# Layer 3's row maximum fused with its masked product, int8 masks from ScalarE, and layer 2's source scores spread through HBM

## The chip, the cores and the metric

The kernel runs on one core of one Trainium2 chip. The metric is the device time of one execution in microseconds (us). All sizes are fixed: a batch of 16 graphs with 1024 nodes each and 128 features a node, in float32.

The names of the engines are those of the profile: PE is TensorE's matrix multiply, PEld its weight load, DVE is VectorE, ACT is ScalarE, POOL is GpSimd, and SP is SyncE, which here issues most of the DMAs. A line number such as L1189 is a line of the kernel before.

## The reference, cut to what matters

Four graph layers in a row, each with a layer norm and a relu ahead of it and a residual sum behind it. `adj` is symmetric in its pattern but not in its values; all its entries are zero or between 0.05 and 1.

```python
# layer 2 (attention by source and destination scores)
h = einsum('bnf,fo->bno', hn, W)
s1 = h @ a[:f]
s2 = h @ a[f:]
alpha = tanh(s1[:, :, None] + s2[:, None, :])
attn = softmax(where(adj > 0, alpha, NEG_INF), axis=-1)
last_h = einsum('bij,bjf->bif', attn, h)

# layer 3 (gated attention)
h = einsum('bnf,of->bno', hn, W_w) + W_b
e = einsum('bil,bkl->bik', h @ A, h)
e = e + swapaxes(e, 1, 2)
att = where(adj > 0, e, 0)
att = softmax(att, axis=1) * adj
h_prime = relu(einsum('bij,bjk->bik', att, h))
...
return o_c * tanh(sigmoid(i_c * h_prime + f_c * hn))
```

Layer 0 is three graph convolutions with cosine weights, and layer 1 a neighbour sum with a two-layer perceptron. They aren't touched by the change.

## The kernel before

**Tiling.** One graph is worked on as 8 blocks of 128 nodes. An adjacency matrix is held as 8 tiles `adjT` of 128 x 1024, transposed while it is loaded (a strided DMA, then a DVE transpose, then an ACT copy that also sums the row). A matrix of 1024 x 1024 scores is made a row of blocks at a time: for block row `j`, `Square.row` computes the upper triangle with matmuls (`sq`, L760) and fills the lower one with TensorE transposes of what ACT copied out before (`above`, L792 and L770), or, for most batches, from a round trip through HBM (`by_hbm` and `got`). Every product is two halves of 512 columns (`HALVES`).

**Layer 3, per row block** (`layer3`, L1136, the loop at L1169). DVE multiplies each half of the scores in PSUM by `adjT > 0` (L1177, `scalar_tensor_tensor` with `is_gt` and `mult`) into a chunk `e`. DVE takes the maximum of the whole row with the sign turned (L1189, `top`). ACT computes exp with that bias and the row's sum (L1193). DVE multiplies by `adjT` (L1202; POOL does it for a few rows of the second last batch, L1198), DVE inverts the sum (L1207), ACT scales the block of features (`hs`, L1211), and TensorE accumulates (L822).

**Layer 2's source scores** (`layer2`, L1028). The projection `h` has 130 columns: 128 features, `s1` and `s2`. ACT's tanh needs `s1` of all nodes along the free dimension, the same on each partition. So TensorE transposes, for each of the 8 blocks, the one column of `s1` broadcast to 128 columns (`along`, L1087 to L1092), and ACT evicts the two halves into `s1` (L1093, through the helper at L622). A branch under a flag "S" that sends the scores through HBM is in the code and not switched on.

**What sets the order.** Nothing is issued as it is written. Each piece of work is recorded as an `Op` with an engine, a price in us, and what it reads and writes. `Plan.order` (L137) then goes through time as a list scheduler would: of the ops that are ready on the engine that can start first, it takes the one with the smallest rank, and it gives buffers their slots. The rank is

```python
lead = self.leads.get(o.key + o.edge, self.leads.get(o.key, 0.0))
o.rank = (self.deadline(o.batch) - o.tail - lead, o.seq)
```

where `tail` is the priced work behind the op and `LEADS` is a table of numbers (L347 to L467) by layer, engine and tile, with extra entries for the first two and the last two batches (`<0`, `<1`, `>1`, `>0`). Ops of a batch may start while an earlier batch is unfinished, up to `AHEAD` = 2 batches. The emitted program is then fixed: each engine runs its own list in order, SP's DMAs among them, and waits on semaphores. `POOLS` and `KINDS` say how many slots each kind of buffer has and how many of them later batches may hold.

`FLAGS` (L264) switches variants; `far` (L523) says for which batches the mirrored half goes through HBM (batches 1 to 13).

Of the kernel before, what the change touches and what calls it, by code (L numbers as in the profile page):

```python
# [9 lines left out]
U8 = mybir.dt.uint8  # L10
AF = mybir.ActivationFunctionType
# [12 lines left out]
FLOOR = 1e-30  # L24

# [197 lines left out]
def tile_adj_preln(  # L223
# [40 lines left out]
    FLAGS = set("CabcdkxhyzTG")  # L264
# [61 lines left out]
    for load_it in first:  # L326
# [11 lines left out]
    POOLS = {"adjT": 16, "adjL": 5, "x": 3, "big": 13, "above": 2, "got": 1, "bank": 8, "small": 29, "row": 6, "hbm": 3, "hrow": 2}  # L338
# [4 lines left out]
        "hrow": ("hrow", 2, 1),  # L343
    }
    PERIOD, LAST, AHEAD, WINDOW = 60.0, 52.0, 2, 0.05

    LEADS = {  # L347
        "0 ACT hT": -1, "0 DVE hn": -8, "0 DVE mv": 42.5, "0 DVE nb": -20, "0 DVE st": -77.5, "0 PE ps": -72.5,
        "0 POOL rstd": -1, "00 ACT above": -10.5, "00 ACT hT": 95, "00 ACT hTn": -20.5, "00 ACT sq": -31,
        "00 DMA by": -13.5, "00 DMA got": 15.5, "00 DVE above": -135, "00 DVE ew": 79.5, "00 DVE h": -95.5,  # L350
        "00 DVE ss": -131.5, "00 PE acc0": -252.5, "00 PE ps": -142, "00 PE psP": -0.5, "00 PE sq": -18.5,
        "00 POOL rn": -129.5, "01 ACT above": 56, "01 ACT hT": 11.5, "01 ACT hTn": 15, "01 ACT sq": 15.5,
        "01 DMA by": 4.5, "01 DMA got": 18.5, "01 DVE above": 4.5, "01 DVE ew": 51.5, "01 DVE h": -2.5,
        "01 DVE ss": 16, "01 PE acc0": -164.5, "01 PE ps": 42, "01 PE psP": -5.5, "01 PE sq": -11,
        "02 ACT above": -2, "02 ACT hTn": -615, "02 ACT sq": -25.5, "02 DMA by": 63.5, "02 DMA got": 0.5,
        "02 DVE above": 43.5, "02 DVE ew": -232.5, "02 DVE ss": 79.5, "02 DVE x": -55.5, "02 PE acc0": -28.5,
        "02 PE ps": 12.5, "02 PE sq": 222, "02 POOL rn": -103, "1 ACT g": -33, "1 ACT hn": 66, "1 ACT y1": -7.5,
        "1 DMA adjL": -113, "1 DVE adjL": -21, "1 DVE hn": 1.5, "1 DVE mv": 237.5, "1 DVE nb": 46,
        "1 DVE st": -625.5, "1 DVE x": -0.5, "1 PE acc1": 4, "1 PE py": -167.5, "1 PE py2": 67,
        "1 POOL rstd": -43, "2 ACT e2": -24, "2 ACT h": 287.5, "2 ACT hfl": 53, "2 ACT hn": -13.5,  # L360
        "2 ACT hnT": 18, "2 ACT s1": -14, "2 DVE alone": -51.5, "2 DVE e2": 48.5, "2 DVE h": 20,
        "2 DVE hn": 48.5, "2 DVE hrow": -43.5, "2 DVE mv": -2.5, "2 DVE nb": 78, "2 DVE rden": 9.5,
        "2 DVE x": 10, "2 PE acc2": 108.5, "2 PE p1": -90, "2 PE pf": -26.5, "2 PE ps": 117.5, "2 PE psP": -315,
        "2 POOL rstd": 4.5, "3 ACT above": -19.5, "3 ACT e3": 96.5, "3 ACT gate": -185.5, "3 ACT h3T": 19.5,
        "3 ACT hn": -84.5, "3 ACT hnT": -9.5, "3 ACT hp": -5, "3 ACT hpT": 41, "3 ACT hs": 46.5, "3 ACT z": 25,
        "3 DMA by": -13.5, "3 DMA got": 0.5, "3 DMA z": -130.5, "3 DVE e3": -363.5, "3 DVE gate": 83,
        "3 DVE h": -111.5, "3 DVE hn": 69, "3 DVE mv": -2, "3 DVE nb": 147, "3 DVE st": -192, "3 DVE sum": 53.5,
        "3 DVE top": -84, "3 DVE z": -925, "3 PE acc3": -130.5, "3 PE pg": -18.5, "3 PE ps": 19,
        "3 PE psN": 114, "3 PE psP": 95, "3 PE sq": -0.5, "3 POOL rstd": -59, "3 POOL z": 0.5,
        "T ACT adjT": 1.5, "T DMA adjT": -140.5, "T DVE adjT": -391, "x DMA x": 54.5, "0 ACT hT <0": -2,  # L370
        "0 ACT hT >1": -4.5, "0 ACT hn <1": -4.5, "0 DVE hn <0": 8.5, "0 DVE hn <1": 8.5, "0 DVE hn >0": 15.5,
        "0 DVE hn >1": 1, "0 DVE mv <0": -4.5, "0 DVE mv <1": 113, "0 DVE mv >0": 47.5, "0 DVE mv >1": -25.5,
        "0 DVE nb <0": 101.5, "0 DVE nb <1": -62.5, "0 DVE nb >0": -49, "0 DVE nb >1": -18.5,
        "0 DVE st <0": -85, "0 DVE st <1": -73.5, "0 DVE st >0": -122.5, "0 DVE st >1": -32, "0 PE ps <0": 85.5,
        "0 PE ps <1": 36, "0 PE ps >0": -31, "0 PE ps >1": 40, "0 POOL rstd <0": -6.5, "0 POOL rstd <1": -26,
        "0 POOL rstd >0": -7, "0 POOL rstd >1": 15.5, "00 ACT above <0": -32, "00 ACT above <1": -88,
        "00 ACT above >0": -294, "00 ACT above >1": -3, "00 ACT hT <0": 147.5, "00 ACT hT <1": -7,
        "00 ACT hT >0": 21, "00 ACT hT >1": 161.5, "00 ACT hTn <0": -70.5, "00 ACT hTn <1": 119.5,
        "00 ACT hTn >0": -22, "00 ACT hTn >1": -11, "00 ACT sq <0": -34, "00 ACT sq <1": 134.5,
        "00 ACT sq >0": -119, "00 ACT sq >1": -25.5, "00 DMA by <1": 0, "00 DMA got <1": 1,  # L380
        "00 DVE above <1": -197, "00 DVE ew <0": 180, "00 DVE ew <1": 13, "00 DVE ew >0": -125,
        "00 DVE ew >1": -147.5, "00 DVE h <0": -25.5, "00 DVE h <1": -4.5, "00 DVE h >0": 12,
        "00 DVE h >1": -50.5, "00 DVE params <0": 171, "00 DVE ss <0": 0, "00 DVE ss <1": -73.5,
        "00 DVE ss >0": -46.5, "00 DVE ss >1": -4, "00 PE acc0 <0": -39.5, "00 PE acc0 <1": -212,
        "00 PE acc0 >0": -327.5, "00 PE acc0 >1": -253.5, "00 PE params <0": 56.5, "00 PE ps <0": -18.5,
        "00 PE ps <1": -16, "00 PE ps >0": -32, "00 PE ps >1": -130.5, "00 PE psP <0": -2.5, "00 PE psP <1": 32,
        "00 PE psP >0": -22.5, "00 PE psP >1": -43, "00 PE sq <0": 28.5, "00 PE sq <1": 10, "00 PE sq >0": 3.5,
        "00 PE sq >1": 10, "00 POOL rn <0": -11, "00 POOL rn <1": -164.5, "00 POOL rn >0": -96.5,
        "00 POOL rn >1": -144, "01 ACT above <0": 113, "01 ACT above <1": -11, "01 ACT above >0": 65.5,
        "01 ACT above >1": 24, "01 ACT hT <0": -15, "01 ACT hT <1": -17.5, "01 ACT hT >0": 3.5,  # L390
        "01 ACT hT >1": -39, "01 ACT hTn <0": 16.5, "01 ACT hTn <1": -22, "01 ACT hTn >0": 68,
        "01 ACT hTn >1": 8, "01 ACT sq <0": 174, "01 ACT sq <1": -3.5, "01 ACT sq >0": -69, "01 ACT sq >1": 107,
        "01 DMA by <1": -9, "01 DMA got <1": 25, "01 DVE above <1": -5, "01 DVE ew <0": 140,
        "01 DVE ew <1": -13.5, "01 DVE ew >0": -9.5, "01 DVE ew >1": -34, "01 DVE h <0": -6, "01 DVE h <1": -6,
        "01 DVE h >0": -4.5, "01 DVE h >1": 43.5, "01 DVE ss <0": -13.5, "01 DVE ss <1": 1,
        "01 DVE ss >0": 17.5, "01 DVE ss >1": 106, "01 PE acc0 <0": -17, "01 PE acc0 <1": -31,
        "01 PE acc0 >0": 10.5, "01 PE acc0 >1": 25.5, "01 PE ps <0": 46, "01 PE ps <1": 51, "01 PE ps >0": -56,
        "01 PE ps >1": 82, "01 PE psP >1": 6, "01 PE sq <0": 0, "01 PE sq <1": -6, "01 PE sq >0": 23.5,
        "01 PE sq >1": -25, "02 ACT above >0": -3.5, "02 ACT hTn <0": -145.5, "02 ACT hTn <1": -452.5,
        "02 ACT hTn >0": -65.5, "02 ACT hTn >1": -373.5, "02 ACT sq <0": -8.5, "02 ACT sq <1": -43,  # L400
        "02 ACT sq >0": -58, "02 ACT sq >1": -22.5, "02 DMA by <1": 47.5, "02 DMA got <1": 4,
        "02 DVE above <1": 36.5, "02 DVE ew <0": -5, "02 DVE ew <1": -72, "02 DVE ew >0": -202.5,
        "02 DVE ew >1": -44, "02 DVE ss <0": 70, "02 DVE ss <1": 60.5, "02 DVE ss >0": 39, "02 DVE ss >1": 58,
        "02 DVE x <0": -115, "02 DVE x <1": -125.5, "02 DVE x >0": 0, "02 DVE x >1": -173.5,
        "02 PE acc0 <0": -46.5, "02 PE acc0 <1": -209, "02 PE acc0 >0": 0, "02 PE acc0 >1": -96.5,
        "02 PE ps <0": -241.5, "02 PE ps <1": -295.5, "02 PE ps >0": -48, "02 PE ps >1": -28,
        "02 PE sq <0": -33.5, "02 PE sq <1": -145, "02 PE sq >0": 89, "02 PE sq >1": 0.5, "02 POOL rn <0": 47.5,
        "02 POOL rn <1": -39, "02 POOL rn >0": -118.5, "02 POOL rn >1": -53, "1 ACT g <0": 23, "1 ACT g <1": 48,
        "1 ACT g >0": 25.5, "1 ACT g >1": -35, "1 ACT hn <0": 57.5, "1 ACT hn <1": 189, "1 ACT hn >0": -5.5,
        "1 ACT hn >1": -4.5, "1 ACT y1 <0": 10.5, "1 ACT y1 <1": 13.5, "1 ACT y1 >0": -26.5,  # L410
        "1 ACT y1 >1": 10.5, "1 DMA adjL <0": -772.5, "1 DMA adjL <1": 0, "1 DMA adjL >0": 39,
        "1 DMA adjL >1": -7.5, "1 DVE adjL <0": 42.5, "1 DVE adjL <1": 201.5, "1 DVE adjL >0": -10.5,
# [1022 lines left out]
```

## Time and profile before

| what | value |
|---|---|
| median of three runs | 2436.25 us (2435.44 to 2436.89) |
| profiled execution, first to last instruction | 2432.9 us |
| mean granted TensorE clock | 0.996 of full speed |
| PE matmuls | 11946 |
| DVE busy, ACT busy, POOL busy | 2107.7, 1288.8, 245.1 us |
| moved by DMA | 263.35 MB, mean 108 GB/s |

How to read it: busy time is the time in which an engine had at least one instruction at work, over the whole span. The matmuls of a trace overlap, and their ends are modelled, so what one costs is read from the distance of two starts. The profile's waits name the instruction that came last before an engine went on; an engine that isn't the bottleneck may wait at no cost. All three runs are within 1.5 us.

### The profile page before, as it was taken

To read this page: it belongs to the slowest core of one execution; us is meant where nothing else is said; L and a number is where in the kernel's file an instruction comes from. 1 tells how busy PE (TensorE), PEld (TensorE's weight loads), DVE (VectorE), ACT (ScalarE), POOL (GpSimd) and SP (SyncE) were. 2 spreads that over 40 slices of the span, in tenths; PEclk is the share of its full clock that TensorE was granted. 3 is DMA by queue.
4 is the path that set the end of the run, shared out by engine and by line. 5 is a ranking of instruction groups with operands and counts; after the bars stand their busy time and mean duration, and the time that the engine had idled before them with its cause. 6 is when DMAs were issued, how large, how long until landed. Compare 5 with 4: busy or idle time off the path is not lost. (4 is left out here: it accounts for less than half of the span.)

```text
span 2432.9 us, 34859 instructions
## 1 busy us (share of the span) xinstructions
PE 2387.8 (98%) x11946; PEld 1589.5 (65%) x11946; DVE 2107.7 (87%) x5264; ACT 1288.8 (53%) x2404; POOL 245.1 (10%) x166
## 2 busy tenths in 40 slices
PE   6999999999999999999999999999999999999996
PEld 3568576675767657676675767757576675765763
DVE  6758989889998988999888998998999888897676
ACT  5316564645646465554744646455454644656275
POOL 3001010100101101010010101001011010100011
PEclk9999999999999999999999999999999999999998
DMA  9531927549295573936639285473936738063000
GB/s 149 111 104 36 173 53 148 130 88 171 62 165 121 103 155 81 166 86 136 142 80 180 53 164 130 92 151 80 165 103 122 155 75 151 18 94 89 27 1 18
DMA packets 1126321, 263.35 MB, mean 108 GB/s; under 512 B 970016, under 2 KB 1109552, under 8 KB 1126144
## 3 DMA queue, kind: packets, MB, share of 16 engines
q1 hardware_dynamic: 1108368, 251.73, 52.9%
q10 hardware_dynamic: 16944, 8.52, 1.2%
q8 instruction: 94, 1.54, 0.3%
q0 software_dynamic: 832, 0.88, 0.3%
q14 instruction: 83, 0.68, 0.1%
HBM read 198.14 MB, written 62.91 MB: 107 GB/s over the span
## 5 line engine op out<-in xcount | busy, mean ns | idle before, releaser
L959 DVE SCALAR_TENSOR_TENSOR ew<-sq,rn,adjT 128x512 f32<-128x512 f32 x612 | 432.3, 739 | 83.3 <-ACT above L792 45.6
L822 PE MATMUL acc<-ew,h 128*128 128x512 f32 x1024 | 477.9, 593 | 2.1 <-DVE ew L959 2.1
L760 PE MATMUL sq<-hTn 128*128 128x512 f32 (+3 forms) x1152 | 432.8, 488 | 0.7 <-DVE above L782 0.4
L792 ACT COPY above<-sq 128x256 f32<-128x256 f32 (+3 forms) x432 | 168.2, 394 | 448.5 <-PE sq L760 248.7
L760 PEld LDWEIGHTS sq<-hTn 128*128 128x128 f32 x1152 | 201.4, 192 | 155.2 <-issue 103.9
L822 PEld LDWEIGHTS acc<-ew,h 128*128 128x128 f32 x1024 | 178.9, 190 | 161.8 <-issue 124.0
L833 PEld LDWEIGHTS acc<-h,ew 128*128 128x128 f32 x2048 | 240.8, 192 | 22.6 <-issue 18.8
L833 PE MATMUL acc<-h,ew 128*128 128x128 f32 x2048 | 250.3, 276 | 0.0
L822 PE MATMUL acc<-e,hs 128*128 128x512 f32 x512 | 242.1, 597 | 5.3 <-DVE e L1202 4.1
L833 PEld LDWEIGHTS acc<-h,e 128*128 128x128 f32 x2048 | 232.9, 192 | 11.9 <-issue 6.5
L833 PE MATMUL acc<-h,e 128*128 128x129 f32 x2048 | 233.8, 275 | 1.2 <-DVE e L1109 1.2
L822 PE MATMUL acc<-adjL,hn 128*128 128x512 f32 x512 | 233.5, 593 | 0.3 <-ACT hn L726 0.3
L562 POOL TENSOR_TENSOR rstd<-ve,mhalf 128x8 f32<-128x8 f32 x64 | 105.2, 1643 | 1237.1 <-DVE ve L681 1237.1
L1193 ACT ACTIVATE e<-e,top 128x1024 f32<-128x1024 f32 x128 | 147.0, 1149 | 133.8 <-DVE top L1189 131.8
L770 PEld LDWEIGHTS sq<-ident,above 128*128 128x128 f32 x960 | 125.7, 141 | 125.6 <-issue 89.0
L890 ACT ACTIVATE adjT<-adjT 128x1024 f32<-128x1024 f32 x128 | 135.0, 1055 | 137.2 <-DVE adjT L887 94.5
L770 PE MATMUL sq<-ident,above 128*128 128x128 f32 x960 | 175.1, 273 | 2.0 <-ACT above L792 2.0
L705 ACT ACTIVATE hn<-x,nb,rstd 128x128 f32<-128x128 f32 x256 | 105.3, 482 | 122.8 <-DVE nb L689 115.2
L1109 DVE SCALAR_TENSOR_TENSOR e<-adjT,e 128x512 f32<-128x512 f32 x256 | 158.8, 681 | 9.3 <-ACT e L1105 8.7
L887 DVE STREAM_TRANSPOSE adjT<-adjT 128x1024 f32<-128x1024 f32 x128 | 154.7, 1224 | 11.7 <-DMA adjT<-in_adj_dram 11.0
L782 DVE STREAM_TRANSPOSE above<-sq 128x512 f32<-128x512 f32 x208 | 146.5, 707 | 17.2 <-PE sq L760 17.1
L1202 DVE TENSOR_TENSOR e<-e,adjT 128x512 f32<-128x512 f32 x248 | 161.2, 681 | 0.0
(149 smaller groups left out, 3512.0 us busy)
## 6 DMA issues: line engine op xcount, KB each, us to landing
adjT<-in_adj_dram SPq DMA_DIRECT2D x512, 128.0 KB, 4.0
adjL<-in_adj_dram SPq DMA_DIRECT2D x128, 512.0 KB, 5.0
by_hbm<-above SPq DMA_DIRECT2D x104, 512.0 KB, 3.7
got<-by_hbm SPq DMA_DIRECT2D x416, 128.0 KB, 3.0
x<-in_x_dram SPq DMA_DIRECT2D x15, 512.0 KB, 4.6
out_dram<-z ACTq DMA_DIRECT2D x15, 512.0 KB, 5.6
x<-in_x_dram SPq DMA_DIRECT2D x2, 256.0 KB, 4.9
out_dram<-z ACTq DMA_DIRECT2D x2, 256.0 KB, 2.2
```

The source lines that it names most:

```text
L760: lambda: nc.tensor.matmul(dst.t[:, (first - lo) * P :], cols(leftT.t, j), span(rightT.t, first, hi), start=True, stop=True),
L770: nc.tensor.transpose(cols(dst.t, r), cols(above.t, p), ident)
L782: lambda: nc.vector.transpose(span(above.t, p, p + 4), read.t),
L792: lambda: nc.scalar.copy(span(above.t, p, p + hi - first), read.t[:, (first - lo) * P :]),
L822: lambda s=s, lo=lo, hi=hi: nc.tensor.matmul(acc[s].t, cols(h.t, at, w), span(ew.t, lo, hi), start=(j == 0), stop=(j == NB - 1)),
L833: nc.tensor.matmul(a.t[:, (c - lo) * n : (c - lo + 1) * n], cols(ew.t, c), h.t[:, at * w : at * w + n], start=(j == 0 and c == lo), stop=( ...
L887: dve(V(N), [t], [t], lambda t=t: nc.vector.transpose(t.t, t.t), True)
L890: lambda t=t, c=c: nc.scalar.activation(t.t, t.t, AF.Copy, accum_out=su.t[:, c : c + 1]),
L959: lambda view=view, ew=ew, rn=rn, j=j, lo=lo, hi=hi: nc.vector.scalar_tensor_tensor(by_block(span(ew.t, lo, hi), D, 4), view(), rn.t[:, j ...
L1109: lambda e=e, j=j, lo=lo, hi=hi: nc.vector.scalar_tensor_tensor(span(e.t, lo, hi), span(aT[j].t, lo, hi), 0.0, span(e.t, lo, hi), op0=ALU. ...
L1193: lambda e=e, top=top, tot=tot: nc.scalar.activation(e.t[:, 0:N], e.t[:, 0:N], AF.Exp, bias=top.t, accum_out=tot.t),
L1202: lambda e=e, j=j, lo=lo, hi=hi: nc.vector.tensor_mul(span(e.t, lo, hi), span(e.t, lo, hi), span(aT[j].t, lo, hi)),
```

## The change

The variants "m" and "r" are switched on, two kinds of buffer are added, and the table of leads is a new one.

```diff
-    FLAGS = set("CabcdkxhyzTG")
+    FLAGS = set("CabcdkxhyzTGmr")
...
-    POOLS = {"adjT": 16, "adjL": 5, "x": 3, "big": 13, "above": 2, "got": 1, "bank": 8, "small": 29, "row": 6, "hbm": 3, "hrow": 2}
+    POOLS = {"adjT": 16, "adjL": 5, "x": 3, "big": 13, "above": 2, "got": 1, "bank": 8, "small": 29, "row": 6, "hbm": 3, "hrow": 2, "mask": 5, "dot": 12}
...
-        "hrow": ("hrow", 2, 1),
+        "hrow": ("hrow", 2, 1), "mask": ("mask", 5, 5), "dot": ("dot", 12, 9),
     }
-    PERIOD, LAST, AHEAD, WINDOW = 60.0, 52.0, 2, 0.05
+    PERIOD, LAST, AHEAD, WINDOW = 60, 52, 2, 0.05
```

*Leads.* Every entry of `LEADS` is replaced. `T`, `x`, `0` to `3` and `00` to `02` stand for the loads and layers; a few entries of each:

```diff
-        "0 ACT hT": -1, "0 DVE hn": -8, "0 DVE mv": 42.5, "0 DVE nb": -20, "0 DVE st": -77.5, "0 PE ps": -72.5,
+        "T DMA adjT": 112, "T DVE adjT": -341, "T ACT adjT": -97, "x DMA x": 338, "0 DVE st": -634.5,
+        "0 DVE mv": 268, "0 POOL rstd": 48, "0 DVE nb": -455, "0 DVE hn": -381.5, "0 ACT hn": -11,
...
```

*Layer 3, for all batches.* ACT turns each row of `adjT` into a mask of 0 and 1 in int8 with two instructions, Sign and then Relu. DVE's masked product becomes one `tensor_tensor_reduce` a half, which multiplies mask and scores, writes `e`, and gives the half's maximum (`peak`). The maximum over 1024 elements becomes one over the two halves' values. `top`, `peak` and `sum` move from the kind `small` to the new kind `dot`.

```diff
+            top = dot(f"top_{b}_{j}", 1)
+            if "m" in FLAGS:
+                mask = Buf("mask", [P, N], f"mask_{b}_{j}")
+                act(
+                    S(N), [aT[j]], [mask],
+                    lambda mask=mask, j=j: nc.scalar.activation(mask.t, aT[j].t, AF.Sign),
+                )
+                act(S(N), [mask], [mask], lambda mask=mask: nc.scalar.activation(mask.t, mask.t, AF.Relu))
+                peak = dot(f"peak_{b}_{j}", 2)
...
+                    dve(
+                        V(HALF) + 0.06, [blk(mask, lo, hi), p], [blk(e, lo, hi), blk(peak, s, s + 1, 1)],
+                        lambda e=e, view=view, mask=mask, peak=peak, s=s, lo=lo, hi=hi: nc.vector.tensor_tensor_reduce(
+                            by_block(span(e.t, lo, hi), D, 4), by_block(span(mask.t, lo, hi), D, 4), view(), 1.0, LOWEST,
+                            op0=ALU.mult, op1=ALU.max, accum_out=peak.t[:, s : s + 1],
+                        ),
+                        p is square.got,
+                    )
...
+                dve(
+                    TINY, [peak], [top],
+                    lambda peak=peak, top=top: nc.vector.tensor_reduce(
+                        top.t, peak.t, axis=AX.X, op=ALU.max, negate=True
+                    ),
+                )
```

*Layer 2, for all batches but the last.* One transpose turns the eight columns of `s1` into 8 rows of 128, ACT copies them to SBUF, SP stores them to HBM (4 KB) and loads them back as one row for all 128 partitions (512 KB written). The loop with the eight transposes and two evictions is then left by a `break`; batch 15 still runs it.

```diff
+        if "r" in FLAGS and b < B - 1:
+            pt, sr = ps(f"pt_{b}"), rowbuf(f"sr_{b}")
+            pe(
+                TR, [h], [pt],
+                lambda: nc.tensor.transpose(pt.t[0:NB, 0:P], by_block(h.t, E2)[:, :, D], ident),
+            )
+            act(S(P), [pt], [sr], lambda: nc.scalar.copy(sr.t[0:NB], pt.t[0:NB, 0:P]))
+            sd = Buf("hrow", [NB, P], f"sd_{b}")
+            op("DMA", 0.2, [sr], [sd], lambda: nc.sync.dma_start(sd.t, sr.t[0:NB]), lat=2.2)
+            op(
+                "DMA", 1.8, [sd], [s1],
+                lambda: nc.sync.dma_start(s1.t[:, 0:N], sd.t.rearrange("c p -> (c p)").partition_broadcast(P)),
+                lat=2.4,
+            )
+        elif "S" in FLAGS and b < B - 2:
...
-            if "S" in FLAGS and b < B - 2:
+            if "r" in FLAGS and b < B - 1 or "S" in FLAGS and b < B - 2:
                 break
```

*Tile types.* When the buffers are made, one of the kind `mask` is int8 and all others stay float32.

## The prediction

> **What bounds the kernel now.** I read the page's first two parts, then the engine-by-engine sums in chosen stretches, then what TensorE waited for, then the groups of instructions, and last the chain that ended last. Page, busy time and slices:
>
> ```profile
> span 2432.9 us, 34859 instructions
> ...
> PE 2387.8 (98%) x11946; PEld 1589.5 (65%) x11946; DVE 2107.7 (87%) x5264; ACT 1288.8 (53%) x2404; POOL 245.1 (10%) x166
> ...
> PE   6999999999999999999999999999999999999996
> DVE  6758989889998988999888998998999888897676
> ```
>
> A busy PE need not be a PE at its peak. The Trainium skill's "Perfetto Trace Analysis" (Tensor Engine Instruction) says that the end of a matmul in a trace is estimated and not observed. So I go by starts. In the timeline eight transposes of layer 2 take
>
> ```profile
> 202.36 1.04 PE L1090 MATMUL p<-ident,h 128*128 128x128 f32 x8
> ```
>
> 1.04 us with the last one's 0.273 included: (1.04 - 0.273) / 7 = 0.110 us from start to start, although each row says 273 ns. The trace bears the page out. In the same way the 512-column matmuls start every 0.43 us in long runs, against a 593 ns mean. Whether there are holes is seen in the stretches (us, then busy us of each engine with instructions):
>
> ```profile
> 0.00:100.00 100.00, 79.45 (x323) 47.23 (x324) 75.44 (x177) 46.18 (x92) 26.34 (x38) 0.97 0.99 158
> ...
> 200.00:2300.00 2100.00, 2098.11 (x10644) 1408.62 (x10644) 1876.41 (x4664) 1134.37 (x2105) 185.41 (x111) 1.00 0.57 113
> ...
> 2388.80:2410.00 21.20, 14.75 (x58) 7.75 (x57) 21.20 (x35) 13.61 (x28) 3.87 (x2) 0.99 0.09 26
> 2410.00:2422.30 12.30, 12.23 (x36) 6.08 (x36) 7.66 (x14) 4.70 (x11) 0.00 (x0) 0.87 0.00 0
> ```
>
> From 200 to 2300 us TensorE lacks 1.9 us of 2100, at full clock. So there only TensorE's own work counts, and DVE and ACT have 10% and 46% to spare. The holes lie at the ends: about 20 us before 100, and the last batch's layer 3, where DVE is busy all of 2388.8 to 2410 and TensorE 14.75 of 21.2. TensorE's waits over the whole span say the same:
>
> ```profile
> PE ps_hT L569 <- DVE hn L698: 17.4, 2, 12.5
> PE acc L822 <- DVE e L1202: 4.1, 3, 2.0
> ...
> PE sq L770 <- ACT above L792: 2.0, 4, 1.1
> ```
>
> 12.5 us of the first are the start of the kernel. The chain that ended last, in order of time, shows the tail row by row:
>
> ```profile
> 2391.77 1.19 DVE e L1177 x2
> 2392.96 1.13 DVE top L1189
> 2394.09 0.07 DVE sum L1207
> ...
> 2409.95 10.39 PE acc L822 x20
> ```
>
> The groups that the change touches:
>
> ```profile
> L1189 DVE TENSOR_REDUCE top<-e 128x1 f32<-128x1024 f32 x128 | 154.6, 1212 | 0.5
> ...
> L1177 DVE SCALAR_TENSOR_TENSOR e<-adjT,sq 128x512 f32<-128x512 f32 x204 | 132.9, 672 | 9.1 <-ACT above L792 6.7 <-PE sq L770 0.8
> ...
> L1105 ACT ACTIVATE e<-e 128x1024 f32<-128x1024 f32 x128 | 133.0, 1052 | 0.1
> ...
> L705 ACT ACT_TABLE_LOAD x1 | 1.3, 1283 | 7.9 <-DMA x<-in_x_dram 7.9
> ```
>
> **What the skill says of the new operations.** The Trainium skill's "ScalarE: Activation LUTs" (Table sets, Precision budgets) says that cheap functions stand in every table set and groups sign with relu, identity and square as exact to one unit; a switch of sets would cost 2.66 us with its drain. The trace has one load of 1.283 us for Relu, Square, Tanh, Exp and Copy together; that Sign joins them no run here shows. The Trainium skill's "VectorE: DVE Perf Modes" (The perf-mode tier table) calls the reduction a one-element-a-cycle op; the row of 1212 ns for 1024 elements agrees. The same page (Two Vector instructions with no wait between them) counts an op that writes out an accumulator as two instructions; DVE shows none here, but ACT's readouts are rows of 0.19 us.
>
> **Part 1, the fused maximum.** Removed: 128 reductions of 1.212 us, 155 us of DVE. The 256 masked products (L1177, 0.67 us) become product plus running maximum. Their cost is not in the trace: the same stream of 512 elements excludes a gain, so +0 below, and +0.19 each above if an accumulator readout comes on top. I take +0.1: 256 x 0.1 = 26 us. Added: 128 maxima of two values, 0.15 us each as the reciprocal L1207's row (19.0 us for 128): 19 us. DVE: 2108 - 155 + 26 + 19 = 1998 us (82%). In the middle this is worth nothing, because TensorE covers it.
>
> In the tail it counts. From 2388.8 to 2417.6 DVE runs 8 rows without a hole. Eight maxima at the chain's 1.13 us go (-9.0), 16 products gain 0.1 (+1.6), eight small maxima come at 0.07 to 0.15 (+0.9): -6.5 us. TensorE's hole in 2388.8 to 2410 is 21.2 - 14.75 = 6.5 us, after which it works through without a stop, so 6.5 is also the most it can gain there.
>
> **Part 2, masks on ScalarE.** Added: 128 rows of Sign and Relu over 1024 elements. Nearest row 1052 ns (f32 to f32). An int8 output could be no cheaper (same elements) or, unknown, somewhat dearer; 1.05 us each: 256 x 1.05 = 269 us. ACT, after part 3: about 1289 + 269 - 15 = 1543 us (63%), covered by TensorE in the middle, as 37% stays free. The new wait: each product now waits for its row's mask; queued behind it on DVE are other batches' ew products and transposes, for which TensorE waits. Five mask buffers let ACT run five rows ahead. In the tail that means: five of the last batch's eight masks fit in before, where ACT stands idle (5.09 us before one eviction at 2371.7), and three rows, 6 us, fall inside. In the stretch from 2388.7 to 2418 ACT has 16.2 us of work, DVE 28.9 and TensorE 22.9; ACT with 6 more has 22.2, against DVE's new 22.4. Three engines of equal load that feed each other will not overlap fully. So of 6.5 us I take 4 (0 to 6.5).
>
> **Part 3, source scores through HBM, batches 0 to 14.** Removed: 8 transposes at 0.110 us, two evictions of 0.62 us (L622 s<-p). Added: one transpose, its streamed side still 128 wide, 0.11 us; one small copy, 0.27 us (as L1067); on SP a 4 KB store and a 512 KB broadcast load. TensorE: 15 x 7 x 0.110 = 11.5 us less, in the middle where nothing else counts: 11.5 us off the time. ACT: 15 x (1.24 - 0.27) = 15 us less. The scores arrive later: for 512 KB the loads of x land after 4.6 us, the smallest store shown (256 KB) after 2.2, together some 7 us against some 1.5 us. The Trainium skill's "DMA: Bandwidth & Descriptors" (Anatomy of one DMA) gives each transfer about 2 us of fixed time; the 2.2 agrees. It is hidden by the neighbouring batches (AHEAD is 2), and batch 15 keeps the old path. On SP the load waits for the store, some 2 to 3 us with prefetches of adjT and got queued behind; the same pair of by_hbm and got already waits 198.6 us in 66 waits there without TensorE feeling it. 7.9 MB more on 263 is 3%.
>
> **Part 4, the order.** Every lead changes, so every queue is reshuffled. In the middle it can hardly gain (1.9 us) but can lose. At the start DVE's transposes wait for adjT with the DMA engines at 0.99, and one hole of 4.9 us at 50 us waits for batch 1's x; the new order may move that either way. I take 0, with -6 to +6.
>
> **Sum.** 2432.9 - 11.5 (transposes) - 4 (tail) + 0 (order) = 2417.4 us of span. The three runs' median, 2436.25, lies 3.35 above the profiled span, which I take as fixed: 2420.8, so **2421 us**. Its own range: tail 0 to 6.5, order -6 to +6: 2412 to 2430.
>
> **Rivals.**
> - *Both ends tighten* (12%). The new order fills the hole at 50 us and the tail's later holes too (2.0 us for hn at 2377, 1.2 for e2 at 2348): -11.5 - 6.5 - 9: 2409. For it: DVE has 110 us less to do. Against: the start waits for DMA, and layer 3 isn't in it.
> - *The gain is given back* (11%). Masks sit in ACT's queue ahead of evictions that TensorE waits for, about 0.12 us a row: 128 x 0.12 = 15 us: 2436, no change.
> - *Slower: ACT's queue becomes the bound* (15%). ACT runs in order; two mask instructions are 2.1 us in front of an `above` copy or an hT eviction. The place is layer 3 of each batch; at 0.3 us of TensorE stall a row it costs 38 us: 2436 - 15 + 38 = 2459. It decides for slower from (15.5 + 4.9) / 128 = 0.16 us a row. For it: ACT already waits 248.7 us for squares just finished, so the copies follow close on TensorE. Against: TensorE now waits 2.0 us in all for such copies. If Sign needed another table set, the loads alone would be 256 x 1.28 = 328 us of ACT, and this case with it.
>
> **How the numbers follow.** The forecast has 62%. A change under 0.2% (4.9 us: 2431.4 to 2441.1) can't be told from none. Faster: 62 + 12 = 74%; same 11%; slower 15%. The range 2406 to 2440 takes in the forecast, the both-ends case and the given-back case.
>
> **What would show it.** Right: TensorE still without holes from 200 to 2300, its matmuls 105 fewer, busy near 2376; products under 0.86 us; DVE near 2000, ACT near 1540; one table load. Wrong: rows where TensorE waits for `above` or ew in the middle, more than 15 us together; DVE waiting for the mask; the tail's DVE rows with holes that end on ACT.

## The result, and the profile after

The changed kernel takes 2452.77 us (median of 4 runs, 2451.12 to 2453.42) where the kernel before takes 2435.85: a ratio of 1.007, 95% interval 1.0058 to 1.0082. It is slower by 17 us, and the prediction had it faster by 15. A line number from here on is one of the changed kernel, unless a run of its own is named; up to the middle of layer 2 it lies 30 higher (L822 of before is L852), behind the new branch 44 and more (L1105 is L1149).

The page of the changed kernel, busy time and slices:

```profile
span 2449.3 us, 35070 instructions
...
PE 2394.4 (98%) x11841; PEld 1579.1 (64%) x11841; DVE 1986.7 (81%) x5520; ACT 1508.6 (62%) x2645; POOL 245.8 (10%) x166
...
PE   7999999999999999999999999999999999999987
...
DVE  7658888887888978888888888878889887895765
```

TensorE has 105 matmuls fewer, as foretold, and yet 6.6 us more busy time. That is the trap of the modelled ends: a matmul's row reaches some 0.16 us past the start of the next, so a hole shorter than that is booked as busy. The same stretches as before show only what is left over:

```profile
0.00:100.00 100.00, 82.86 (x331) 48.85 (x332) 76.01 (x178) 55.00 (x103) 26.30 (x38) 0.98 1.05 158
200.00:2300.00 2100.00, 2090.28 (x10423) 1383.97 (x10422) 1756.62 (x4854) 1321.64 (x2304) 183.59 (x110) 1.00 0.64 117
```

Before, TensorE lacked 1.9 us of the 2100; now it lacks 9.7, and DVE has become emptier (1756.6 against 1876.4 us). TensorE is held up, and by an engine that has more room than before.

Starts tell how much. For each pair of neighbouring matmuls in the trace I take the distance of their starts less the shortest distance that such a matmul shows in a long run (0.429 us for a pass of 512 columns, 0.215 for 256, 0.110 for a transpose). The excess is a stall, the rest is work. A stall is mostly waiting, but it also holds matmuls at half clock: at the ends of both kernels the trace shows stretches of 3.4 or 6.8 us with a granted clock of 0.50, and one of 3.4 us adds some 1.5 us. Neither kernel has one between 100 and 2300 us. In us:

| | first start | work | stalls to 100 | stalls 100 to 2300 | stalls after 2300 | last start to end | span |
|---|---|---|---|---|---|---|---|
| before | 12.5 | 2366.1 | 16.4 | 7.4 | 19.5 | 10.9 | 2432.9 |
| changed | 11.4 | 2354.5 | 14.2 | 33.4 | 24.2 | 11.7 | 2449.3 |
| difference | -1.1 | -11.6 | -2.2 | +26.0 | +4.7 | +0.8 | +16.4 |

So the work fell by what was promised, and 26 us of stalls came in the middle, where nothing had been lost before. Sorted by the matmul that came late, the 33.4 us are: 17.2 before an accumulation with VectorE's product `ew` (4.2 before the change), 15.4 in layer 0's chain from `psP` over `ps_hTn` to `sq<-hTn` (1.7), and 0.8 elsewhere (1.5).

TensorE's waits in the changed kernel (engine and line, what it waited for, us in total, times, longest) name the first half:

```profile
PE ps_hT L599 <- DVE hn L728: 11.6, 2, 11.4
PE acc L852 <- DVE e L1272: 9.0, 5, 2.3
PE acc L852 <- DVE ew L989: 7.2, 9, 2.2
PE acc L863 <- DVE e L1153: 6.0, 2, 5.2
...
PE acc L863 <- DVE ew L989: 1.2, 3, 0.7
```

The two rows on `ew` lie in the middle, with 8.4 us together; before there were 0.9 us of such waits there. They are fewer than the 17.2 because the rows hide the short holes. And VectorE's own waits in the changed kernel say what it stood at before `ew`:

```profile
DVE ew L989 <- DMA got<-by_hbm: 18.6, 15, 4.3
...
DVE e L1231 <- ACT above L822: 15.4, 20, 3.7
```

That wait for `got` was 1.9 us in 4 waits before. It is not among VectorE's largest (it waits 56.0 us for `hp` with no harm), but it is the one that TensorE stands behind. Here it is on SP's queue in the middle of the changed kernel:

```profile
1016.77 3.60 SPq L843 DMA_DIRECT2D got<-by_hbm  x4
1020.46 8.48 SPq L909 DMA_DIRECT2D adjT<-in_adj_dram  x8
1028.99 0.61 SPq L832 DMA_DIRECT2D by_hbm<-above  x1
1029.70 0.52 SPq L890 DMA_DIRECT2D adjL<-in_adj_dram  x1
1033.08 2.32 SPq L843 DMA_DIRECT2D got<-by_hbm  x4
```

and on VectorE and TensorE in the same microseconds:

```profile
1038.95 2.08 DVE L989 SCALAR_TENSOR_TENSOR ew<-got,rn,adjT 128x512 f32<-128x512 f32 x3 [1.07 <-DMA got<-by_hbm]
...
1039.75 1.13 PE L852 MATMUL acc<-ew,h 128*128 128x512 f32 x2 [0.75 <-DVE ew L989]
```

The last VectorE transpose into `above` ended at 1017.8. Its store waited 11.2 us on SP behind the rest of a copy back and two tiles of `adjT`, eight issues. It was issued at 1028.99, its copy back began at 1033.08, and VectorE could go on at 1038.95: 9.96 us for the round trip. The code prices that trip at 0.7 + 2.2 us for the store and 3.6 + 2.4 us for the copy, 8.9 us. The order gave it those 8.9 us and no more (VectorE was there at 1037.88, 8.89 us after the issue), so VectorE, which takes its instructions in order, stood for 1.07 us, and TensorE behind it for 0.75. Ten more stores after 100 us stood more than 5 us on SP; before the change none did.

The second half is seen in one chain. The changed kernel at layer 0's second product, TensorE and VectorE:

```profile
1051.51 2.04 PE L630 MATMUL psP<-w,hT 128*128 128x128 f32 x16
...
1052.70 2.16 DVE L674 SCALAR_TENSOR_TENSOR h<-psP,rn,b 128x128 f32<-128x128 f32 x8 [1.78 <-PE psP L630]
...
1053.62 1.63 PE L599 MATMUL ps_hTn<-ident,h 128*128 128x128 f32 x8
```

and the kernel before at the same place:

```profile
1047.45 1.05 PE L600 MATMUL psP<-w,hT 128*128 128x128 f32 x8
...
1048.89 2.33 DVE L644 SCALAR_TENSOR_TENSOR h<-psP,rn,b 128x128 f32<-128x128 f32 x8
...
1049.01 1.05 PE L600 MATMUL psP<-w,hT 128*128 128x128 f32 x8
...
1050.57 0.60 PE L569 MATMUL ps_hTn<-ident,h 128*128 128x128 f32 x4
...
1051.46 0.60 PE L569 MATMUL ps_hTn<-ident,h 128*128 128x128 f32 x4
```

Before, other work stands between the halves, and each four transposes run through in 0.60 us. Now the 16 matmuls run back to back, and the eight transposes take 1.63 us instead of 1.04: each waits some 0.15 us for VectorE's next block of `h`. No such hole is long enough to be shown as idle.

What the change put in has the expected prices. Groups of the changed kernel (line, engine, operation, count, then busy us and mean ns, then idle time ahead):

```profile
L1231 DVE CUSTOM_DVE_ANT_0 e<-mask,sq 128x512 f32<-128x512 int8 x204 | 135.2, 675 | 25.9 <-ACT above L822 15.4 <-PE sq L800 9.6 <-PE sq L790 0.6
L1220 ACT ACTIVATE mask<-adjT 128x1024 int8<-128x1024 f32 x128 | 134.4, 1052 | 18.8 <-DVE peak L1231 18.7
L1222 ACT ACTIVATE mask<-mask 128x1024 int8<-128x1024 int8 x128 | 132.6, 1049 | 0.4
...
L1231 DVE DVE_READ_ACCUMULATOR2_ANT peak<- 128x1 f32 x256 | 21.1, 82 | 0.0
L1252 DVE TENSOR_REDUCE top<-peak 128x1 f32<-128x2 f32 x128 | 18.4, 147 | 1.7
...
L735 ACT ACT_TABLE_LOAD x1 | 1.3, 1283 | 7.3 <-DMA x<-in_x_dram 7.3
```

### The profile page after: what moved, and what is told of

Same layout as the page of the kernel before. It is cut to its first block, busy times and chain, and to the rows that moved or that the text cites. A ratio compares the mean times of both kernels' runs of the same rounds, so it can differ in the third digit from the quotient of the medians.

```text
span 2449.3 us, 35070 instructions
## 1 busy us (share of the span) xinstructions
PE 2394.4 (98%) x11841; PEld 1579.1 (64%) x11841; DVE 1986.7 (81%) x5520; ACT 1508.6 (62%) x2645; POOL 245.8 (10%) x166
## 4 chain that ended last, share of the span: by engine, by line
PE 83%; DMA 5%; SPq 4%; DVE 4%; ACT 2%; issue 1%; POOLq 0%; POOL 0%; DVEq 0%; ACTq 0%
PE acc L852 32%; PE sq L790 17%; PE acc L863 17%; PE psP L630 6%; PE sq L800 4%; SPq L909 3%; DMA by_hbm<-above 2%; DMA got<-by_hbm 2%; PE ps_hTn L599 2%; DVE ew L989 2%; SPq L843 1%; PE py L1051 1%; PE pg L640 1%; PE py L640 1%; PE ps_hnT L599 1%
## 5 line engine op out<-in xcount | busy, mean ns | idle before, releaser
L852 PE MATMUL acc<-ew,h 128*128 128x512 f32 x1024 | 481.9, 595 | 7.3 <-DVE ew L989 7.2
L822 ACT COPY above<-sq 128x384 f32<-128x384 f32 (+3 forms) x432 | 167.5, 392 | 457.2 <-PE sq L790 250.3
L852 PEld LDWEIGHTS acc<-ew,h 128*128 128x128 f32 x1024 | 179.0, 191 | 175.2 <-issue 133.2
L852 PE MATMUL acc<-e,hs 128*128 128x512 f32 x512 | 244.3, 599 | 9.0 <-DVE e L1272 9.0
L852 PE MATMUL acc<-adjL,hn 128*128 128x512 f32 x512 | 230.9, 592 | 0.0
L852 PEld LDWEIGHTS acc<-adjL,hn 128*128 128x128 f32 x512 | 94.2, 190 | 106.2 <-issue 97.1
L812 DVE STREAM_TRANSPOSE above<-sq 128x512 f32<-128x512 f32 x208 | 144.8, 705 | 20.8 <-PE sq L790 20.7
L1231 DVE CUSTOM_DVE_ANT_0 e<-mask,sq 128x512 f32<-128x512 int8 x204 | 135.2, 675 | 25.9 <-ACT above L822 15.4
```

The source lines that it names most:

```text
L812: lambda: nc.vector.transpose(span(above.t, p, p + 4), read.t),
L822: lambda: nc.scalar.copy(span(above.t, p, p + hi - first), read.t[:, (first - lo) * P :]),
L852: lambda s=s, lo=lo, hi=hi: nc.tensor.matmul(acc[s].t, cols(h.t, at, w), span(ew.t, lo, hi), start=(j == 0), stop=(j == NB - 1)),
L1231: lambda e=e, view=view, mask=mask, peak=peak, s=s, lo=lo, hi=hi: nc.vector.tensor_tensor_reduce(by_block(span(e.t, lo, hi), D, 4), by_blo ...
```

## The experiments

Four theories. A: the round trip `above`, `by_hbm`, `got` comes back too late for the order. B: ScalarE is too full with the masks. C: the s1 round trip loads SP and the DMA engines. D: the pieces are sound, and the new order as a whole loses what they gain. All results in one table; the stalls and the work are taken from starts as above, and "ew" and "chain" are the two halves of the middle. Each ratio is to the kernel before, run on the same chip.

| run | median us | ratio (95%) | work | stalls to 100 | middle (ew, chain) | after 2300 |
|---|---|---|---|---|---|---|
| changed | 2452.8 | 1.0070 (1.0058 to 1.0082) | 2354.5 | 14.2 | 33.4 (17.2, 15.4) | 24.2 |
| store_first | 2447.9 | 1.0054 (1.0042 to 1.0067) | 2354.5 | 14.0 | 27.6 (10.5, 15.4) | 24.5 |
| sign_only | 2450.1 | 1.0065 (1.0051 to 1.0079) | 2354.5 | 13.1 | 33.6 (17.3, 15.4) | 21.2 |
| s1_pool_queue | 2461.9 | 1.0115 (1.0100 to 1.0130) | 2354.5 | 13.1 | 43.2 (11.7, 16.9) | 23.0 |
| after_reordered | 2443.2 | 1.0036 (1.0024 to 1.0047) | 2354.5 | 12.5 | 30.5 (6.4, 14.1) | 20.0 |
| before_reordered | 2442.1 | 1.0032 (1.0019 to 1.0045) | 2366.1 | 7.2 | 24.7 (3.5, 5.4) | 20.8 |
| after_slack | 2438.1 | 1.0011 (1.0003 to 1.0019) | 2354.5 | 12.3 | 31.1 (4.1, 11.5) | 15.3 |
| before_slack | 2449.1 | 1.0062 (1.0048 to 1.0075) | 2366.1 | 11.0 | 23.5 (2.4, 14.3) | 19.9 |
| after_act | 2425.4 | 0.9961 (0.9947 to 0.9974) | 2354.5 | 9.4 | 19.7 (1.8, 10.3) | 16.0 |
| after_act2 | 2420.1 | 0.9934 (0.9922 to 0.9947) | 2354.5 | 9.7 | 13.6 (2.2, 11.4) | 16.7 |
| before_act | 2430.1 | 0.9980 (0.9972 to 0.9988) | 2366.1 | 10.5 | 7.2 (1.6, 3.3) | 19.8 |
| late_store | 2422.7 | 0.9950 (0.9937 to 0.9964) | 2354.5 | 8.5 | 18.9 (2.2, 11.3) | 14.4 |
| one_pass_act2 | 2419.4 | 0.9936 (0.9923 to 0.9950) | 2354.5 | 9.5 | 13.5 (2.2, 11.4) | 14.6 |

**store_first.** The late stores, alone, go ahead of the `adjT` fetches.

```diff
     ordered = plan.order()
+    for o in [o for o in ordered if o.engine == "DMA" and o.key.endswith(" by")]:
+        at = ordered.index(o)
+        homes = {(t.pool, t.slot) for t in o.new}
+        while ordered[at - 1] not in o.preds and not ordered[at - 1].key.endswith(" got") and not homes & {(t.pool, t.slot) for t in ordered[at - 1].bufs}:
+            at -= 1
+        ordered.remove(o)
+        ordered.insert(at, o)
```

> The changed kernel with one thing moved: on SP's queue each store of above into by_hbm goes ahead of the adjT fetches that stand between it and the copies that it reads. Nothing is left out. Theory A (the round trip above, by_hbm, got comes back too late, VectorE waits for it in order, TensorE waits behind): in the middle batches one store in four was issued 9.8 to 11.2 us after its tile was ready; it now goes at once and got comes 3 us earlier, so VectorE's wait for got falls from 18.6 us to about 9 (the stores that were not late keep theirs), TensorE's stalls at sq to acc<-ew fall by some 7, and the time goes from 2452 to 2442 to 2446. Theory B (ScalarE is too full with the masks) and theory C (the s1 round trip loads SP and the DMA engines): no change, 2450 to 2454, and VectorE's wait for got moves elsewhere on it.

VectorE's waits of this run, and its SP queue at the place shown above:

```profile
DVE ew L989 <- DMA got<-by_hbm: 8.6, 10, 1.5
```

```profile
1020.41 0.90 SPq L832 DMA_DIRECT2D by_hbm<-above  x1
1021.40 8.42 SPq L909 DMA_DIRECT2D adjT<-in_adj_dram  x8
...
1030.64 3.93 SPq L843 DMA_DIRECT2D got<-by_hbm  x4
```

The wait fell to 8.6 us, and the stalls before `ew` from 17.2 to 10.5; the chain's 15.4 did not move at all. The median fell by 4.9 us, some 2 us short of the expected range; the runs of the two kernels just touch (2444.9 to 2451.8 against 2451.1 to 2453.4). The place of those stores is thus some 5 of the 17 us; theory A is right and too small.

**sign_only.** In each mask the second pass emits nothing; the order is the changed kernel's.

```diff
-                act(S(N), [mask], [mask], lambda mask=mask: nc.scalar.activation(mask.t, mask.t, AF.Relu))
+                act(S(N), [mask], [mask], lambda mask=mask: None)
```

> The changed kernel in its own order with the second pass of each mask left out: Relu after Sign is not issued, so 128 ScalarE passes of 1.05 us are gone (the adjacency has no negative entries, so the mask is the same). Theory B (ScalarE too full): its queue is 134 us shorter, hT and above are evicted sooner, and 10 us or more of the 26 us of new stalls in the middle go: 2435 to 2443. Theory A (the got round trip is late): ScalarE is not on that path, at most 2 us: 2449 to 2454. Theory C: no change.

134 us less of ScalarE left the middle as it was, 33.6 us. Theory B would have had 10 us or more. The 2.6 us between the medians can't be told from nothing: the interval holds the changed kernel's ratio.

**s1_pool_queue.**

```diff
-            op("DMA", 0.2, [sr], [sd], lambda: nc.sync.dma_start(sd.t, sr.t[0:NB]), lat=2.2)
+            op("DMA", 0.2, [sr], [sd], lambda: nc.gpsimd.dma_start(sd.t, sr.t[0:NB]), lat=2.2)
...
-                lambda: nc.sync.dma_start(s1.t[:, 0:N], sd.t.rearrange("c p -> (c p)").partition_broadcast(P)),
+                lambda: nc.gpsimd.dma_start(s1.t[:, 0:N], sd.t.rearrange("c p -> (c p)").partition_broadcast(P)),
```

> The changed kernel in its own order with the store sd and the broadcast load s issued by GpSimd in place of SP. Nothing is left out. Theory C (SP standing at sd and s for 95 and 22 us holds up what is queued behind it): by_hbm, adjT and adjL are issued up to 6 us a batch earlier, the wait for got goes, and the time falls by 8 us or more: 2436 to 2444. Theory A: the late stores stand behind adjT fetches and not behind s, so the time stays within 3 us: 2449 to 2455. Theory B: no change. Above 2455 the GpSimd queue itself is slow to issue them, and nothing follows.

SP no longer stood 95 and 22 us for these two, and yet the time rose by 9 us, and TensorE's waits for `above` from 1.2 to 12.5 us (1 wait to 11). The trace shows how, here at one of the 11 places:

```profile
1055.27 0.55 POOL L1110 DMA_DIRECT2D s<-sd  x1 [2.87 <-PE ps_hTn L599]
1060.19 1.15 ACT L1145 ACTIVATE e<-s,h 128x1024 f32<-128x1024 f32 x1 [2.83 <-DMA s<-sd]
1061.25 0.46 ACT L822 COPY above<-sq 128x384 f32<-128x384 f32 x1
1061.76 0.33 PE L800 MATMUL sq<-ident,above 128*128 128x128 f32 x1 [1.72 <-ACT above L822]
```

GpSimd issued the load 3.8 us after the copy `sr` had ended, where SP took 1.9 us, so the scores came later. ScalarE's tanh stood for them (26.9 us in 14 waits; 1.1 us in 3 in the changed kernel), the copy of `above` stood behind it in ScalarE's queue, and TensorE behind that. The order gives this round trip no slack either: in the changed kernel the tanh of the same place waits 0.18 us. What SP's relief is worth by itself this run can't tell, and theory C's DMA traffic was not taken away by itself.

**after_reordered and before_reordered.** If neither stores nor masks nor s1 account for the loss, the order as a whole is to be tried. Both kernels keep their instructions, slots and prices, and take a written-out order. It was made by moving single operations by a few places within their engine's queue and keeping what shortened the time that the planner's prices add up to, with the two transfers at the trace's values.

```diff
     ordered = plan.order()
+    ordered = [ordered[int(i)] for i in ORDER.split()]
```

> The changed kernel with every instruction, buffer slot and price as it is, and only the order of the work within each engine's queue changed: from the plan's order, single operations were moved by a few places on their own engine wherever that shortened the planner's sum, with the by_hbm and got transfers priced at what this trace shows for them (0.6 us and then 3.4 us for the store, 2.4 us and then 3.9 us for the copy back). Nothing is left out. Theory D (the loss is in the new order and not in the new pieces): TensorE's work stays at 2354.5 us, its stalls in the middle fall from 33.4 us to about 12 and at the end from 24 to 15 to 20, and the time goes from 2452 to 2415 to 2432, below the kernel before. Theories B and C (the masks' ScalarE passes or the s1 round trip slow the engines whatever the order): the middle keeps 25 us or more of stalls and the time stays above 2443.

> The control: the kernel before, with the same moves of single operations within the queues by the same rule and the same prices, and nothing else. It shows how much of the gain of the other run is the moves' and would have been had without the change. TensorE's work stays at 2366.1 us; its stalls of 16.4, 7.4 and 19.5 us leave at most some 15 us: 2420 to 2433. Theory D with sound pieces: it stays above the reordered changed kernel by up to the 11.5 us of transposes that the change saves. If the pieces of the change cost more than the transposes save, it comes out below it.

The expected 2415 to 2432 was missed: 2443.2. And the control got slower by 7 us. A tight order on paper is not one on the chip. (Of the control's 24.7 us in the middle, 4.4 lie in three stretches at half clock.) Two things were wrong with the rule, and the traces show both. The first is the missing slack: VectorE still waited 18.3 us for `got` in after_reordered. The second came out one pair later.

**after_slack and before_slack.** The same diff, with another ORDER, whose moves had to be good also with late transfers.

> The changed kernel with every instruction, buffer slot and price as it is, and again only the order within the queues moved, operation by operation, but now with room for the transfers: the moves had to keep the planner's sum short also when a by_hbm store lands 3.4 us after its issue, a got copy 4.1 us after its last issue, an adjT fetch holds SP for 4.24 us and x lands after 6.5 us. Nothing is left out. Theory D with its cause (the order leaves the by_hbm and got round trip no slack): VectorE's wait for got falls from 18.3 us in the tight reordering to under 6, TensorE's middle stalls from 30.5 us to under 18, and the time from 2443 to 2418 to 2432, below the kernel before. If the round trip is not the cause, slack for it buys nothing: 2440 or more, with 25 us or more left in the middle.

> The control: the kernel before with its queues moved by the same rule with the same room for the transfers. The tight reordering cost it 7 us, with 24.7 us of stalls in the middle. Theory D: with slack the middle falls back to under 12 us and the time to 2422 to 2434; the difference to the changed kernel under the same rule is then what the pieces are worth, up to the 11.7 us of TensorE work they save. If the round trip is not the cause: 2438 or more.

The stalls before `ew` fell to 4.1 us, so the slack did what it was for; but others took their place (15.5 us outside of both halves), and the control rose to 2449. ScalarE's waits in before_slack show the second fault:

```profile
ACT e L1515 <- DMA out_dram<-z: 8.7, 3, 3.5
```

and its timeline one instance:

```profile
917.76 0.42 ACTq L1727 DMA_DIRECT2D out_dram<-z  x1
...
922.13 1.15 ACT L1515 ACTIVATE e<-s,h 128x1024 f32<-128x1024 f32 x1 [2.37 <-DMA out_dram<-z]
```

The plan books the store of `z` with SP's DMAs; the code issues it from ScalarE (L1727 here). The tanh of the next layer 2 (`e<-s,h`) takes over the buffer that this store reads, and stands in ScalarE's queue behind it. No wait of ScalarE for that store is seen in the kernel before or in the changed kernel; in the four reordered ones it waits 4.2 to 15.7 us.

**after_act, after_act2 and before_act.** The same rule with that store in ScalarE's order.

> The changed kernel, its instructions, slots and prices untouched, only the order within the queues moved once more, from the order of after_slack, with the room for the transfers kept and one thing added: the store of z to the output is issued by ScalarE in its own order, and the earlier moves had it priced as if SP issued it. In after_slack ScalarE waited 14.0 us for that store where the two original kernels never do. Theory D: those waits go, the middle falls from 31.1 us to under 20 and the time from 2438 to 2418 to 2430, below the kernel before. If the pieces themselves hold the middle up (theories B and C), it stays at 25 us or more and the time at 2435 or more.

> The same rule and prices as after_act with the moves started from the changed kernel's own order: a second order of the same pieces, to see how much of a result is the order's luck. Theory D: also 2418 to 2432. If only one of the two gains, luck in the order is as large as the effect.

> The control: the kernel before, moved from its own order by the same rule with the same prices. In its earlier reorderings ScalarE waited 11 to 16 us for the store of z, and the time rose by 7 and 14 us. Theory D: with that mended it is no slower than the kernel before, 2422 to 2435, and it stays above after_act by up to the 11.7 us of TensorE work that the change saves. If the pieces are worth nothing, it is level with after_act or below.

Now both orders of the changed kernel beat the kernel before, and the better one, 2420.1 us, is the fastest that leaves nothing out. The control gains 5 us. Between these two orders the change is worth 10 us: 2430.1 to 2420.1. That is one order on each side and no property of the pieces alone: under the first rule the pair was level (2443.2 and 2442.1), under the second 11 us apart, and after_act is only 4.7 us below before_act.

The 5 us between the two orders of the changed kernel are not bare luck. ScalarE's waits for the store of `z` fell to 0 in after_act2, but to 4.1 us in after_act (3.3 in before_act), and after_act's one wait is seen again on TensorE:

```profile
611.59 1.15 ACT L1571 ACTIVATE e<-s,h 128x1024 f32<-128x1024 f32 x1 [4.10 <-DMA out_dram<-z]
...
614.55 5.67 PE L1289 MATMUL acc<-h,e 128*128 128x129 f32 x27 [4.09 <-DVE e L1579]
```

The stall is 4.3 us, and the clock stands at 0.50 from 612.5 to 619.3 us, which costs another 2.5 us. Together they are 6.8 us, more than the 6.1 by which the middles differ (19.7 and 13.6).

The page and the stretch of after_act2:

```profile
span 2418.7 us, 35226 instructions
...
PE 2379.5 (98%) x11841; PEld 1580.0 (65%) x11841; DVE 1990.2 (82%) x5520; ACT 1501.4 (62%) x2645; POOL 247.1 (10%) x166
```

```profile
100.00:2300.00 2200.00, 2200.00 (x11028) 1465.92 (x11028) 1839.47 (x5099) 1353.98 (x2382) 198.27 (x118) 1.00 0.65 116
```

```profile
DVE ew L1415 <- DMA got<-by_hbm: 5.7, 2, 3.5
```

The same instructions as in the changed kernel, no less DMA load (0.65 against 0.62 there), ScalarE as full: and in the middle TensorE shows no idle time at all, only 13.6 us of holes too short to show. So a full ScalarE and the s1 round trip don't make the loss by themselves, as theories B and C have it; theory D is shown for the 20 us by which the order alone brings the middle down. Another 6.4 us of stalls remain above the control's 7.2, most of them in the chain; what makes these is open (see below).

**late_store and one_pass_act2.** Two checks on after_act2. The first puts 31 stores behind one or two `adjT` fetches again; of its loop only the core is shown.

```diff
+            if q.engine == "DMA" and q.key.split()[-1] in ("by", "got"):
+                break
+            if q.engine == "DMA" and q.key.endswith(" adjT"):
+                past, to = past + 1, k
+                if past == 2:
+                    break
+        ordered.remove(o)
+        ordered.insert(to, o)
```

> The reverse of store_first, on the good order: after_act2 with its by_hbm stores put behind the next one or two adjT fetches on SP's queue wherever such fetches come before the store's own copy back (31 of 104 stores, two or three a batch). Nothing else is moved and nothing left out. Theory A: a store behind two fetches is issued up to 8.5 us later, got comes later by what slack there was not, VectorE's wait for got rises from 5.7 us to 20 or more and the time from 2420 to 2430 or more. If late stores are only a sign of a bad order and not a cause, 2418 to 2424.

> after_act2 with the second pass of each mask (Relu after Sign) left out, 134 us less on ScalarE; the mask is the same on this non-negative adjacency. If the masks are covered where the order is good, within 3 us of after_act2, 2417 to 2423. If ScalarE's load still costs (theory B), 2414 or less.

late_store missed theory A's 2430: 2422.7 us, and VectorE's waits for `got` are 8.4 us in all, not 20; the stalls before `ew` stayed at 2.2. But the middle rose from 13.6 to 18.9 us, and one of the 31 stores makes nearly all of it. In this order it was too late for layer 3:

```profile
698.64 0.69 DVE L1657 CUSTOM_DVE_ANT_1 e<-mask,got 128x512 f32<-128x512 int8 x1 [5.00 <-DMA got<-by_hbm]
...
700.94 1.62 PE L1216 MATMUL sq<-h3T,gT 128*128 128x384 f32 x2 [2.52 <-DVE ew L1415]
```

VectorE stood 5.00 us, the product `ew` that TensorE waited for was behind it, and the matmuls after the hole ran at half clock from 700.9 to 704.3 us: 2.7 and 1.8 us of stalls. So a late store on SP costs nothing where the order has slack, as with nearly all of the 31, and costs time where it has none. In the changed kernel, at the place shown, the VectorE product that needs it was put at the very end of the priced round trip. one_pass_act2 came out level (2419.4), so the masks' second pass is covered there.

## Why the prediction was wrong

**TensorE's work: right.** 15 x 7 x 0.110 = 11.5 us was foretold, 11.6 us is measured from starts in every pair of runs.

**The prices: right, nearly all.** The fused product: +0.1 us on 0.67 was taken, 0.675 us plus a readout of 0.082 was found. The small maximum: 0.15 taken, 0.147 found. Sign and Relu to int8: 1.05 taken, 1.052 and 1.049 found, with one table load of 1.283 us, so that Sign stands with the others. VectorE 1998 foretold, 1986.7 found; ScalarE 1543 foretold, 1508.6 found. Of these 34 us, 29 are overlap: the lengths of ScalarE's rows add up to 248.6 us more than before, near the 254 of the prediction, but neighbouring rows overlap more, and busy time counts the overlap once. No product shows a wait for its mask.

**Part 3's later scores: right that they are hidden.** The broadcast lands 3.8 us after its issue, and ScalarE waits 1.1 us in all for it; s1_pool_queue shows that there is no room to spare. On SP the load's wait for the store is 1.5 us a batch where 2 to 3 were taken; the store's own wait for `sr`, 6.3 us a batch, was not thought of. Moving both to GpSimd brought no gain.

**The tail: right in itself, not in this order.** 4 us of gain was taken. From the first product of the last batch's layer 3 to the end, TensorE's stalls fell from 9.9 us to 6.7, and from before_act to after_act2 from 9.5 to 2.3. (The prediction's limit of 6.5 us was read from busy time, which leaves out short holes and matmuls at half clock.) But all stalls after 2300 us rose by 4.7; between before_act and after_act2 they fell by 3.1. One hole makes most of the loss, layer 2 of the last batch, where ScalarE works through tanh and exp and nothing else was put behind for TensorE:

```profile
2349.91 1.06 ACT L1149 ACTIVATE e<-e 128x1024 f32<-128x1024 f32 x1
...
2351.00 1.29 DVE L1153 SCALAR_TENSOR_TENSOR e<-adjT,e 128x512 f32<-128x512 f32 x2 [4.12 <-ACT e L1149]
2351.84 2.49 PE L863 MATMUL acc<-h,e 128*128 128x129 f32 x10 [5.17 <-DVE e L1153]
```

It stays in every order of the changed kernel (4.9 to 5.9 us); the kernel before has at most 2.2 us there. The moves of single operations didn't fill it.

**Part 4, the order: the step that failed.** "I take 0, with -6 to +6." It measured +28.5 us of stalls with the tail in it (-2.2 at the start, +26.0, +4.7), and some 32 us if layer 3's own gain of 3.2 is set apart as the prediction did. With it fell the assumption of parts 1 and 2 that in the middle TensorE covers VectorE and ScalarE: their totals left room, but the order made TensorE wait for single products. The text saw that the middle "can hardly gain (1.9 us) but can lose", and then gave the loss the size of the gain. The bound had to be one-sided and wide. The profile of before held a warning: TensorE lacked 1.9 us of 2100 although VectorE waited there in many places. That is an order that fits, and so little is what a good fit leaves, not a property of the pieces. Of the signs that the prediction named for being wrong, one came out: "more than 15 us together" of TensorE waiting for `above` or `ew` in the middle. By starts it is 17.2 us before `ew` alone; the rows of the profile show 8.4 for both. Two experiments give the size of a misfit: the kernel before itself, in two other orders, lost 7 and 14 us. That after_act2 comes out at 2420.1, next to the forecast of 2421, is partly luck: the work is as foretold and the stalls after 2300 us fell by 2.8 where 4 were taken, but those at the start moved by -6.7 us and those in the middle by +6.2, where the forecast had nothing. (The forecast's own range adds up to 2412 to 2431, not 2430.)

**The rival on the slower side: right side, wrong mechanism.** 2452.8 is near its 2459 by luck: the loss didn't come through the masks in ScalarE's queue; sign_only and one_pass_act2 speak against it.

What stays open: why the chain in layer 0 keeps 10 us or more of stalls in all orders of the changed kernel. The kernel before shows 1.7 to 5.4 us there in three orders and 14.3 in a fourth, but of that 14.3 some 9.4 us are a few large holes before `sq`. The small holes between the transposes `ps_hTn` cost 4.9 to 7.2 us in every order of the changed kernel and nothing in any order of the kernel before. They came with the new plan; whether through its coarse order, which moves by a few places don't undo, or through the slots that it gave out, no run separates. Nor were parts 2 and 3 run each alone.

## What to carry to other kernels

Where the bounding engine has no holes, the order is a tuned part like any other, and a new one is a cost with one sign: bound it by what other orders of the same pieces lose, not by zero plus or minus. Judge an idea in an order that was fitted to it, and run the old kernel through the same fitting as a control: here that turns "17 us slower" into "10 us faster", with the best order found on each side. When a planned order loses on the chip, look for the transfer whose priced round trip ends exactly where an in-order engine needs it, and for the DMA that the plan books on another queue than the one that issues it.

## What the runs showed of the hardware

- The custom VectorE instruction with a maximum as its accumulator brings a second instruction, a readout of 82 ns, on top of a stream of the same length as the plain product (675 against 672 ns).
- ScalarE's int8 costs neither more nor less than float32: 1052 ns for 1024 elements f32 to int8, 1049 ns int8 to int8, 1052 ns f32 to f32.
- TensorE's busy time can rise while its work falls: holes under about 0.16 us between matmuls are hidden in their rows. In the changed kernel most of the chain's 15.4 us lay in such holes, and only distances of starts show them.
- A fetch of `adjT` in squares (128 KB an issue) held SP for 1.06 us an issue in a run of eight (8.48 us; the median of all 512 issues is 0.84 us), where the plain loads of `adjL` with 512 KB took a median of 0.37 us.
- A hole of TensorE can cost more than its length. The 14 traces show 48 times a granted clock of 0.50 for 3.4 or 6.8 us before the last matmul, and each time at least 2.4 us of stalls lie in the 10 us before. One of 3.4 us cost some 1.5 us. Not every hole brings it: three of 2.5 to 2.9 us in before_slack had none.
